# Values by seven products in sequences 2 to 7, earlier sums, gates on ScalarE's queue and look-up masks on ScalarE

## The chip, the cores and the metric

The kernel runs on one core of one Trainium2 chip. The metric is the device time of one execution in microseconds (us); several runs are given with their median, and one more execution was recorded by the hardware profiler. The engines are named as in the profile: PE (TensorE's matmuls), PEld (its weight loads), DVE (VectorE), ACT (ScalarE), POOL (GpSimd), SP (SyncE, which here only issues DMAs). Each engine works through its own instructions in the order of the program; semaphores hold it where it needs another's result. ACT also issues some DMAs, in its own order.

## The reference

Eight sequences of 1024 rows of 512 are normalized. One branch is a linear attention with three decays and a gate; the other is a feed-forward net whose weights are drawn from a table of 16 values by given indices. All is float32.

```python
xn = (x - mean) / sqrt(var + 1e-5)                 # x: (8, 1024, 512)
# attention
q = xn @ Wq                                        # 128 columns
gate = softmax(xn @ Wg)                            # 3 columns
for i in range(3):
    k = xn @ Wk[i]; v = xn @ Wv[i]                 # 128 columns each
    w = decay[i] ** max(diff - 1, 0) * (diff > 0)  # diff = column - row
    blended += gate[:, i] * (((q @ k.T) * w) @ v)
s = blended @ Wo * out_scale
# feed-forward, weights lut[idx]
h = silu(xn @ lut[gate_idx].T) * (xn @ lut[up_idx].T)   # 1376 columns
g = silu(h @ lut[down_idx].T)
out = x + s * g
```

## The kernel before

The kernel has two phases. `phase_1` makes xn transposed (stored to `xs_d`), the whole attention up to `blended` (stored to `bl_d`), and the feed-forward weights from the indices (stored to `quad_d`, `wd_d` and others). `phase_2` does the feed-forward net, the last attention matmul and the output. The change acts in phase 1; of phase 2 only one look-up (`left_weights`) uses an edited function.

**The order.** `phase_1` walks the sequences b = 0 to 8. In round b it runs side by side, as generators: `project(b)` (called `newer`), the rest of `project(b - 1)` (`ending`), `chunks(b - 1)` (`older`), the look-ups of `ffn_weights` (`build_some`), and the loads of the next sequence (`following`). A round has eight *chunk steps* k = 0 to 7, and a step has three *parts*, each beginning with `tick()`, in which issues put off by `defer(parts, ...)` come due. The order in which the generators are called is the order of every engine's instructions: `keep_order` ties it down. The order of calls in a step is: part 1: newer, older, one building step; part 2: (k < 4: ending twice), newer, one or two building steps, older, three or four building steps, (k < 4: ending); part 3: newer, older.

**project(b).** In step k it transposes one chunk of 128 rows, c = 7 - k, on PE (tile `pt`, L452) and ACT copies it to `xnT` (L453). For the coming chunks ACT normalizes (L446, L447) and gathers statistics (tile `junk`, L436, L437; for k up to 4). `values(c)` multiplies a chunk with the 387 columns of `wvg_sb` (three value matrices and the gates' three columns) in four matmuls into `pv`, which ACT copies to `v_sb` (L459, L462). The profile shows each float32 matmul as two instructions.

`features(hf)` computes q and the three k for half hf (512 rows) with seven products in place of eight, Strassen's way in Winograd's form: sums of blocks of xnT (`t1` to `t4` in `ts_`, by DVE) and of the weights (`sums_of_weights`, by GpSimd, once) are multiplied, and partial results are carried on inside PSUM: ACT copies bank pa to pb, product 6 adds onto pb, ACT copies pb to pc, products 7 and 4 add onto pc. The order is 1, 5, 6, 2, 7, 3, 4, and a product is 8 instructions of 256 columns (L520). The four banks pa, pb, pe, pc have one buffer each. Half 1 runs in steps 4 to 7 of round b (products 1 and 5 in parts 2 and 3 of step 4), half 0 in steps 0 to 3 of round b + 1 as `ending`. Three more banks (`p_c`) go round among pt, pk, psc, pv and po.

`softmax(hf)` makes the gates of a half on DVE and ACT. They must come to lie as rows repeated over all 128 partitions: they are stored to `gT_d` and read back with a broadcast into `ga` (L498). For all halves but one SP stores them two parts later, element by element (`write`, L483: 1536 words); for half 1 of sequence 0 PE transposes them, ACT copies the result to `gs` and issues the store (`turn`, L487 to L491). SP issues the read six parts after the softmax.

**chunks(b).** In step k, for chunk c = 7 - k: PE transposes k (pk, L670), ACT scales the copies (ks, L673); PE makes the scores psc (L677), DVE masks them (pr, L679) and multiplies the next chunk's gates with its q (`gated`, L652); PE adds to the state pu (L687) and makes the output po (L701: first the state's part, then pr's); ACT copies po to bl (L702), pu to R (L708) and decays pu (L715). After steps 3 and 7 ACT issues the store of bl (L704). Step 0 has no state yet, and step 7 leaves none.

**Look-ups.** `look_up` turns a tile of indices, mostly 128 x 1024, into weights. DVE makes three masks from bits 1 to 3 of the index (L220), spreads bit 0 over the word (L223, in place), makes eight leaves (L227), each a pair of table values selected by bit 0, and joins them in a tree of seven predicated copies (L244). Every instruction is one building step. The tree's other operand lies in tiles `leaf1` to `leaf3`.

Of the kernel before, what the change touches and what calls it, by code (L numbers as in the profile page):

```python
# [17 lines left out]
P = 128  # L18
# [30 lines left out]
def recurrent_block(ctx: ExitStack, tc, x, wq, wk, wv, wo, wg, decay_logits, out_scale, lut, gidx, uidx, didx, out):  # L49
# [33 lines left out]
    NQ = NO // 4  # L83
    EPS = 1e-5
# [24 lines left out]
    def more_weights(wvg_sb, wqk_sb):  # L109
        nc.scalar.dma_start(out=wvg_sb[:, :, NI * D :], in_=wg.rearrange("(c p) d -> p c d", p=P))  # L110
        for i in range(NI):
            nc.scalar.dma_start(
                out=wvg_sb[:, :, i * D : (i + 1) * D], in_=wv[i].rearrange("(c p) d -> p c d", p=P)
            )
# [36 lines left out]
    nc.gpsimd.memset(nhalf, -0.5)  # L151

# [8 lines left out]
    zero = const.tile([NI, P], F32)  # L161
# [7 lines left out]
    def tables(room):  # L169
# [8 lines left out]
        nc.gpsimd.memset(e_c, float(P))  # L178
        nc.gpsimd.memset(zero, 0.0)
# [35 lines left out]
    def look_up(build, dst, iv, rows, n):  # L215

        bits = [build.tile([P, n], U8, name=f"bit{j}", tag=f"bit{j}") for j in (1, 2, 3)]
        low = iv.bitcast(U8).rearrange("p (n four) -> p n four", four=4)[:, :, 0]
        for j in (1, 2, 3):
            nc.vector.tensor_scalar(bits[j - 1][:rows, :n], low, 1 << j, None, ALU.bitwise_and)  # L220
            yield
# [14 lines left out]
        def tree(o, level, k):  # L236
            if level == 0:
                leaf(o, k)
                yield
                return  # L240
            t = build.tile([P, n], F32, name=f"leaf{level}", tag=f"leaf{level}")
            yield from tree(o, level - 1, k)
            yield from tree(t[:rows, :n], level - 1, k + (1 << (level - 1)))
            nc.vector.copy_predicated(o, bits[level - 1][:rows, :n], t[:rows, :n])  # L244
            yield
# [3 lines left out]
    def ffn_weights(build, pool, pair_pool):  # L249
# [10 lines left out]
        def gate_up(o):  # L260
# [17 lines left out]
            yield from look_up(build, wf[:, :n], idx[:, :n], P, n)  # L278
# [40 lines left out]
        def down_tail():  # L319
# [5 lines left out]
            yield from look_up(build, wf[:m, :V], idx[:m, :V], m, V)  # L325
            defer(2, lambda: nc.sync.dma_start(out=wdt_d, in_=wf[:m, :V]))

        def down(rows, e):
# [5 lines left out]
            yield from look_up(build, t[:, : 2 * V], idx, P, 2 * V)  # L334
# [67 lines left out]
    def project(b, pools, sides, kept):  # L402
# [5 lines left out]
        xp, xnp, tp, att = pools  # L408
        wvg_sb, wqk_sb, wqs = sides
        xnT = xnp.tile([P, NV, T], F32, name=f"xnT{b}", tag="xnT")  # L410
        mean, rstd, shift = (small.tile([P, NC], F32, name=f"{k}{b}", tag=k) for k in ("mean", "rstd", "shift"))
        v_sb = att.tile([P, NC, NI * D + NI], F32, name=f"v{b}", tag="v")
        gt = v_sb[:, :, NI * D :]
# [9 lines left out]
        def statistics(c):  # L423
# [10 lines left out]
            else:  # L434
                junk = small.tile([P, V], BF16, name=f"junk{b}_{c}", tag="junk", bufs=1)
# [19 lines left out]
        def values(c):  # L455

            pv = p_c.tile([P, NI * D + NI], F32, name=f"pv{b}_{c}", tag="c")
            for v in range(NV):
                nc.tensor.matmul(  # L459
                    pv, lhsT=xnT[:, v, ts(c, P)], rhs=wvg_sb[:, v, :], start=(v == 0), stop=(v == NV - 1)  # L460
                )
            nc.scalar.copy(v_sb[:, c, :], pv)  # L462

        def softmax(hf):
# [15 lines left out]

            def write():
# [3 lines left out]
            def turn():  # L485
# [3 lines left out]
                gs = small.tile([n * NI, P], F32, name=f"gs{b}_{hf}", tag="gs", bufs=1)  # L489
# [3 lines left out]
            ga = gates[-1]  # L493
# [4 lines left out]
            defer(6, lambda: nc.sync.dma_start(out=ga, in_=there.partition_broadcast(P)))  # L498

        def features(hf):  # L500
# [14 lines left out]
            pa, pb, pe, pc = (p_a.tile([P, 2, H], F32, name=f"{r}{b}_{hf}", tag=r) for r in ("pa", "pb", "pe", "pc"))  # L515
# [12 lines left out]

            there = xs_d[b][:, :, ts(hf, H)]
            nc.vector.tensor_tensor(t1, b12, b11, ALU.subtract)  # L530
            yield
            product(pa, 1, True)
            nc.scalar.copy(pb, pa)
            nc.vector.tensor_tensor(t2, b22, t1, ALU.subtract)
            nc.sync.dma_start(out=there[:, 0:4, :], in_=xnT[:, :, ts(2 * hf, H)])
            yield
            product(pe, 5, True)
            nc.scalar.copy(c21, pe)
            nc.vector.tensor_tensor(t3, b22, b12, ALU.subtract)
            nc.sync.dma_start(out=there[:, 4:8, :], in_=xnT[:, :, ts(2 * hf + 1, H)])  # L540
            yield
            product(pb, 6)
            nc.scalar.copy(pc, pb)
            nc.scalar.copy(c12, pb)
            nc.vector.tensor_tensor(t4, b21, t2, ALU.subtract)
            defer(2, lambda: nc.sync.dma_start(out=there[:, 8:16, :], in_=ts_.rearrange("p a b u -> p (a b) u")))
            yield
            product(pa, 2)
            nc.scalar.copy(c11, pa)
            yield  # L550
            product(pc, 7)
            nc.vector.tensor_tensor(c22, pc, c21, ALU.add)
            yield
            product(pe, 3)
            nc.vector.tensor_tensor(c12, pe, c12, ALU.add)
            yield
            product(pc, 4)
            nc.scalar.copy(c21, pc)
            yield
# [25 lines left out]
        yield  # L585
        before = 2 if b == 0 else 3
        lag = 1 if b == 0 else 0
        for k in range(NC):
# [8 lines left out]
            if b == 0 and k == 0:  # L597
                warm_up(5)
            yield
            if k == NC // 2:  # L600
# [7 lines left out]
            half = softmax(1) if k == NC // 2 else iter(())  # L608
# [3 lines left out]
            if k >= lag:  # L612
# [4 lines left out]
        of_half = features(0)  # L617
        for k in range(NC // 2):
            yield
# [10 lines left out]
    def sums_of_weights(wqk_sb, wqs):  # L630

        a11, a12, a21, a22 = (wqk_sb[:, 2 * v : 2 * v + 2, ts(j, 2 * D)] for j in (0, 1) for v in (0, 1))
        s1, s2, s4 = (wqs[:, k] for k in range(3))
# [5 lines left out]
    def chunks(b, pools, kept):  # L639
# [6 lines left out]
        state = None  # L646

# [12 lines left out]
        for c in reversed(range(NC)):  # L660
# [22 lines left out]
            if not first:  # L683


                for i in range(NI):
# [3 lines left out]
                        rhs=v_sb[:, c, ts(i, D)],  # L690
# [853 lines left out]
```

## Time and profile before

| what | value |
|---|---|
| runs | 2084.59, 2086.72, 2086.76 us; median 2086.72 |
| profiled execution | 2085.11 us; span of its instructions 2083.3 us |
| granted clock of PE | 1.000 |
| PE busy, 0 to 600 us | 591.84 us |
| DVE busy, 0 to 600 us | 492.11 us |
| ACT busy, 0 to 600 us | 380.70 us |
| POOL busy, 0 to 600 us | 300.72 us |
| masks, L220 | 48 in phase 1, 0.69 us median |
| copies of pv, L462 | 64, 0.486 us each |
| store of the gates by SP, L483 | 15 |
| read of the gates, L498 | 16, 768 KB each, 7.1 us to landing (median) |

Round 2 begins at 117.68 us, round 3 at 190.87, round 8 at 550.56. A row of the timeline gives start, duration, engine, line, operation, output and inputs, shapes and count; what stands in brackets is the idle time just before, with what ended it. The ends of matmuls are modelled and overlap: what one takes from the next is read from the distance of two starts. A row of busy times gives the stretch and its length and then, for PE, PEld, DVE, ACT and POOL, the busy time and in brackets the number of instructions; at the end stand granted clock, DMA share and GB/s. A row of waits gives the engine and line that waited, what it waited for, the total, the number of times and the longest.

### The profile page before, as it was taken

What the parts mean: (1) busy time and instruction counts of PE and PEld (TensorE: products, weight loads), DVE (VectorE), ACT (ScalarE), POOL (GpSimd) and SP (SyncE); (2) the same over time, 40 slices, a digit from 0 to 9 for tenths busy, and PEclk for the clock granted to TensorE, in tenths of its full rate; (3) what the DMA queues carried; (4) which work ended last, traced back from release to release, by engine and by line L of the source; (5) the groups of instructions that cost most, each with busy time, mean ns of one, the idle gap of its engine ahead of it and who ended that gap; (6) DMA issues with size and microseconds to landing.
All of it is one profiled execution on the core that took longest, in us unless ns stands there. A gap on an engine that the chain in (4) does not pass through costs nothing.

```text
span 2083.3 us, 32914 instructions
## 1 busy us (share of the span) xinstructions
PE 2068.4 (99%) x12043; PEld 1755.3 (84%) x12043; DVE 1462.5 (70%) x2246; ACT 944.1 (45%) x2133; POOL 1043.8 (50%) x1042
## 2 busy tenths in 40 slices
PE   9999999999999999999999999999999999999999
PEld 7887888788888888897888888888978888797887
DVE  8989898788458775675577557656755765675567
ACT  4767766676444424423442442344144324423531
POOL 4554665244356446516543751755275255627442
PEclk9999999999999999999999999999999999999999
DMA  9866778756764734463464447345544734464442
GB/s 231 157 176 181 188 192 178 202 126 185 168 225 154 249 142 155 168 243 133 155 228 160 154 154 261 129 160 192 198 153 153 261 129 151 170 232 144 150 162 104
DMA packets 178494, 367.23 MB, mean 176 GB/s; under 512 B 37871, under 2 KB 113278, under 8 KB 178334
## 3 DMA queue, kind: packets, MB, share of 16 engines
q1 hardware_dynamic: 161734, 338.11, 53.0%
q10 hardware_dynamic: 12120, 12.34, 1.9%
q0 software_dynamic: 4480, 14.68, 1.7%
q8 instruction: 96, 1.57, 0.3%
q14 instruction: 64, 0.52, 0.1%
HBM read 285.36 MB, written 79.73 MB: 175 GB/s over the span
## 4 chain that ended last, share of the span: by engine, by line
PE 92%; DVE 5%; DMA 2%; issue 1%; ACT 0%; SPq 0%; POOL 0%; ACTq 0%; DVEq 0%; POOLq 0%
PE s L963 34%; PE pv L459 6%; PE sE L963 6%; PE s11d L1226 5%; PE s12d L1226 5%; PE s21d L1226 5%; PE po L701 3%; PE pd L1344 3%; PE ps L1351 3%; PE sEd L1226 2%; PE pe L520 2%; PE fs L875 2%; PE pc L520 2%; PE pa L520 2%; PE psc L677 2%; PE pu L687 1%
## 5 line engine op out<-in xcount | busy, mean ns | idle before, releaser
L963 PE MATMUL s<-xs,wq 128*128 128x256 f32 x3264 | 731.6, 379 | 0.6 <-DVE s L986 0.6
L963 PEld LDWEIGHTS s<-xs,wq 128*128 128x128 f32 x3264 | 619.3, 190 | 96.8 <-issue 7.6
L986 DVE TENSOR_TENSOR s<-s,e 128x512 f32<-128x512 f32 x136 | 95.1, 699 | 188.9 <-ACT s L985 188.9
L1315 POOL TENSOR_TENSOR cu<-cu 128x256 f32<-128x256 f32 x32 | 35.1, 1097 | 328.7 <-DVE cl L1314 328.7
L459 PE MATMUL pv<-wvg_sb,xnT 128*128 128x387 f32 x512 | 177.4, 488 | 0.0
L848 POOL TENSOR_TENSOR xs<-xs 128x256 f32<-128x256 f32 x224 | 171.1, 790 | 8.5 <-PE fr L890 4.0
L990 DVE TENSOR_TENSOR sE<-s,e 128x512 f32<-128x512 f32 x136 | 95.0, 699 | 103.2 <-PE s L963 103.1
L1058 POOL TENSOR_TENSOR u<-u,e 128x512 f32<-128x512 f32 x64 | 81.7, 1299 | 147.7 <-DVE u L1054 129.2
L981 ACT COPY e<-sE 128x512 f32<-128x512 f32 x136 | 79.6, 585 | 139.6 <-PE sE L963 137.1
L963 PE MATMUL sE<-xs,wq 128*128 128x256 f32 x544 | 139.6, 379 | 0.0
L459 PEld LDWEIGHTS pv<-wvg_sb,xnT 128*128 128x128 f32 x512 | 94.2, 190 | 53.7
L1062 POOL TENSOR_TENSOR h<-h,u 128x512 f32<-128x512 f32 x64 | 81.1, 1288 | 108.1 <-DVE u L1069 108.1
L438 POOL TENSOR_SCALAR rstd<-rstd 128x1 f32<-128x1 f32 x56 | 26.1, 467 | 209.8 <-ACT junk L437 208.8
L974 ACT COPY s<-s 128x512 f32<-128x512 f32 x136 | 77.5, 570 | 110.2 <-PE s L963 105.1
L985 ACT COPY s<-s 128x512 f32<-128x512 f32 x136 | 77.5, 570 | 97.5 <-PE s L963 97.5
L1226 PE MATMUL s12d<-wdd,z 128*128 128x128 f32 x896 | 118.4, 275 | 0.6 <-ACT s12d L1248 0.6
L963 PEld LDWEIGHTS sE<-xs,wq 128*128 128x128 f32 x544 | 103.4, 190 | 14.1
L1226 PEld LDWEIGHTS s12d<-wdd,z 128*128 128x128 f32 x896 | 109.0, 192 | 0.8 <-ACT s12d L1248 0.8
L227 DVE TENSOR_SCALAR leaf<-idx,lut_x,lut_sb 128x1024 int32<-128x1024 int32 (+2 forms) x119 | 107.7, 930 | 0.0
L656 POOL TENSOR_TENSOR qb<-ga,q_tab 128x384 f32<-128x384 f32 x56 | 75.4, 1346 | 56.1 <-DVE ga L652 26.4
L244 DVE COPY_PREDICATED leaf<-bit,leaf 128x1024 f32<-128x1024 uint8 (+2 forms) x68 | 93.5, 1375 | 1.7
L1355 POOL TENSOR_TENSOR gx<-gx,cu 128x512 f32<-128x512 f32 x32 | 40.7, 1277 | 82.0 <-DVE cu L1353 64.5
(272 smaller groups left out, 4554.4 us busy)
## 6 DMA issues: line engine op xcount, KB each, us to landing
wq<-quadd SPq DMA_DIRECT2D x112, 896.0 KB, 4.5
wdd<-wdd SPq DMA_DIRECT2D x56, 896.0 KB, 5.0
xs<-xsd SPq DMA_DIRECT2D x56, 512.0 KB, 6.4
wq<-quadd SPq DMA_DIRECT2D x48, 448.0 KB, 3.8
x<-in_x SPq DMA_DIRECT2D x64, 256.0 KB, 6.3
xsd<-xnT SPq DMA_DIRECT2D x32, 512.0 KB, 10.9
xsd<-ts SPq DMA_DIRECT2D x16, 1024.0 KB, 16.1
gx<-in_x SPq DMA_DIRECT2D x64, 256.0 KB, 6.4
```

The lines of the kernel that those rows point to most:

```text
L227: nc.vector.tensor_scalar(o.bitcast(I32), iv, lut_x[:rows, k, :], lut_i[:rows, k, 0:1], ALU.bitwise_and, ALU.bitwise_xor,)
L244: nc.vector.copy_predicated(o, bits[level - 1][:rows, :n], t[:rows, :n])
L459: nc.tensor.matmul(pv, lhsT=xnT[:, v, ts(c, P)], rhs=wvg_sb[:, v, :], start=(v == 0), stop=(v == NV - 1))
L520: nc.tensor.matmul(ps[:, j, :], lhsT=lhs[k][:, v, ts(j, D)], rhs=rhs[k][:, v, :], start=start and j == 0 and v == 0, stop=False, skip_grou ...
L848: nc.gpsimd.tensor_tensor(o, x1, x2, ALU.subtract)
L963: nc.tensor.matmul(self.t[n][:, ts(a, H)], lhsT=self.w[:, a, (0, 1, 6, 3, 4, 5, 2)[i - 1], :], rhs=self.xs[:, X_OF[self.ks[a]], D_OF[i], : ...
L981: nc.scalar.copy(self.e, self.t[3])
L986: nc.vector.tensor_tensor(self.t[1], self.t[1], self.e, ALU.add)
L990: nc.vector.tensor_tensor(self.t[3], self.t[2], self.e, ALU.add)
L1058: nc.gpsimd.tensor_tensor(o[:, n], o[:, n], other[:, n], ALU.add)
L1062: nc.gpsimd.tensor_tensor(of_h(half, n), of_h(half, n), two(other[:, n]), ALU.mult)
L1226: nc.tensor.matmul(self.t[n][:, ts(a, P)], lhsT=self.lhs[i][:, e, ts(a, P)], rhs=self.w[:, e, D_OF[i], :], start=start and a == 0 and e == ...
```

## The change

From half 1 of sequence 2 on (`by_sevens = b >= SEVENS`), the values are computed like q and k, by seven products. A half's four chunks times the padded 388 columns of `wvg_sb` are split into blocks of 256 rows, 256 of the contraction and VW = 194 columns; the sums of xnT are those of q and k, the sums of the weights are made once on GpSimd after step 0 of round 2 (with the pad column set to zero). The gates' columns now stand first, so that they are done after product 3. Products of values (v) and of q and k share the four banks, in the order v1, v5, v6, v2, v3, v7, qk1, v4, qk5, qk6, qk2, qk7, qk3, qk4. The steps are spread so: step 4 (or 0): v1 in part 1, v5 in part 2, v6 and v2 at the end of part 2 (half 0) or in part 3 (half 1); next step: v3, v7, qk1; next: v4, qk5, then qk6 and qk2; last: qk7, qk3, qk4. The main loop calls `ending` once in part 1 and twice in part 2.

The sums t1 and t2 are issued one part or more ahead of the first product, and the stores of xnT and of the sums follow v1, v5 and v6. The softmax runs after v3 and v7; after v4 the gates are turned on PE in every such half, stored by ACT, and read back by a DMA that ACT issues, one part later, in place of SP.

In every look-up (all sequences) DVE makes only the mask of bit 1. The other masks are borders: ACT computes max(index - n, 0) for n = 3, 11 and 7 into bytes, and the tree's second level takes the one of its side. The tree's level 1 writes into the unused half of the weights' tile in place of `leaf1`. Besides, `zero`, `gs` and `junk` move or shrink to make room.

```diff
-    def look_up(build, dst, iv, rows, n):
+    def look_up(build, dst, iv, rows, n, spare=None):
-        bits = [build.tile([P, n], U8, name=f"bit{j}", tag=f"bit{j}") for j in (1, 2, 3)]
+        second, *over = [build.tile([P, n], U8, name=f"bit{j}", tag=f"bit{j}") for j in range(4)]
         low = iv.bitcast(U8).rearrange("p (n four) -> p n four", four=4)[:, :, 0]
-        for j in (1, 2, 3):
-            nc.vector.tensor_scalar(bits[j - 1][:rows, :n], low, 1 << j, None, ALU.bitwise_and)
+        nc.vector.tensor_scalar(second[:rows, :n], low, 2, None, ALU.bitwise_and)
+        for j in range(3):
+            nc.scalar.activation(over[j][:rows, :n], iv, AF.Relu, bias=below[:rows, j : j + 1])
             yield
...
+            mask = second if level == 1 else over[2] if level == 3 else over[k // 4]
+            nc.vector.copy_predicated(o, mask[:rows, :n], t[:rows, :n])
...
         def softmax(hf):
+            def spread():
+                (nc.scalar if by_sevens else nc.sync).dma_start(out=ga, in_=there.partition_broadcast(P))
...
-                gs = small.tile([n * NI, P], F32, name=f"gs{b}_{hf}", tag="gs", bufs=1)
+                gs = chk.tile([n * NI, P], F32, name=f"gs{b}_{hf}", tag="ks")
                 nc.scalar.copy(gs, pg)
                 nc.scalar.dma_start(out=there, in_=gs)
...
+            if by_sevens:
+                yield
+                turn()
+                defer(1, spread)
+                yield
+                return
...
         def features(hf):
+            def product_of_v(ps, k, start=False):
+                for m in range(2):
+                    for v in range(2):
+                        nc.tensor.matmul(
+                            ps[:, m, :],
+                            lhsT=rhs[k][:, v, ts(m, P)],
+                            rhs=w_of_v[k][:, v, :],
...
+            def step(k, multiply, width, to):
+                pa, pb, pe, pc = (lambda r=r: bank(r, width) for r in ("pa", "pb", "pe", "pc"))
+                o11, o12, o21, o22 = to
+                if k == 1:
+                    multiply(pa(), 1, True)
+                    nc.scalar.copy(pb(), pa())
+                elif k == 5:
+                    multiply(pe(), 5, True)
+                    nc.scalar.copy(o21, pe())
+                elif k == 6:
+                    multiply(pb(), 6)
+                    nc.scalar.copy(pc(), pb())
+                    nc.scalar.copy(o12, pb())
+                elif k == 2:
+                    multiply(pa(), 2)
+                    nc.scalar.copy(o11, pa())
+                elif k == 7:
+                    multiply(pc(), 7)
+                    nc.vector.tensor_tensor(o22, pc(), o21, ALU.add)
+                elif k == 3:
+                    multiply(pe(), 3)
+                    nc.vector.tensor_tensor(o12, pe(), o12, ALU.add)
+                else:
+                    multiply(pc(), 4)
+                    nc.scalar.copy(o21, pc())
...
+                first = [(k, product_of_v, VW, to) for k in (1, 5, 6, 2, 3, 7, 4)]
+                steps = first[:6] + steps[:1] + first[6:] + steps[1:]
+                half = softmax(hf)
+                after = {4: half, 5: half, 7: half}
...
         for k in range(NC):
...
+            if by_sevens and k >= NC // 2:
+                next(of_half)
+            yield
+            if by_sevens:
+                if k >= NC // 2:
+                    some_of(of_half, 1)
+                yield
+                if k >= NC // 2:
+                    some_of(of_half, 2 - k % 2)
+                if k % (NC // 2) == NC // 2 - 1:
+                    of_half = features(NC // 2 // k)
+                    next(of_half)
+                yield
+                continue
...
     def phase_1():
+                    if k < NC // 2 and b > SEVENS:
+                        next(ending, None)
...
-                        for _ in range(2):
+                        for _ in range(1 if b > SEVENS else 2):
                             next(ending, None)
...
+                    if (b, k) == (SEVENS, 0):
+                        nc.gpsimd.memset(wvg_sb[:, :, NI * D + NI :], 0.0)
+                        sums_of_weights(wvg_sb, wvs, VW)
```

## The prediction

> **What bounds the kernel now.** I read the totals of the page first, then busy time by stretches, then the timeline of single chunk steps, then the waits.
>
> ```profile
> PE 2068.4 (99%) x12043; PEld 1755.3 (84%) x12043; DVE 1462.5 (70%) x2246; ACT 944.1 (45%) x2133; POOL 1043.8 (50%) x1042
> ...
> L459 PE MATMUL pv<-wvg_sb,xnT 128*128 128x387 f32 x512 | 177.4, 488 | 0.0
> ```
>
> TensorE (PE) is busy 2068.4 of 2083.3 us at full granted clock, and it never idles in front of the values (0.0). The kernel is bound by the matmuls themselves: work taken off PE shows one for one, and so does each wait put on PE. Phase 1 ends near 602 us; the edit acts there. Busy time by sequence (its round begins where its first transpose does), columns PE, PEld, DVE, ACT, POOL:
>
> ```profile
> 190.87:263.79 72.92, 71.50 (x412) 59.35 (x411) 67.38 (x83) 49.97 (x132) 38.12 (x35) 1.00 0.69 186
> ...
> 335.35:408.23 72.88, 71.42 (x412) 59.13 (x411) 54.34 (x82) 49.85 (x132) 30.90 (x34) 1.00 0.90 209
> 408.23:479.15 70.92, 70.92 (x412) 59.29 (x411) 57.48 (x78) 49.78 (x132) 34.98 (x35) 1.00 0.62 157
> ```
>
> Sequence 6 (the third row) runs without a PE gap: 70.92 us is the cost of a sequence's matmuls. The others of 2 to 7 last 73.19, 72.92, 71.56, 72.88 and 71.41: 7.4 us of waits in all. ScalarE (ACT) works 50 us of 71, VectorE (DVE) 67 in sequences 2 to 4 and 51 to 57 later. Now chunk step 4 of sequence 6, where the second half's products begin:
>
> ```profile
> 443.85 0.60 PE L452 MATMUL pt<-ident,x 128*128 128x128 f32 x4
> 444.05 0.27 ACT L702 COPY bl<-po 128x128 f32<-128x128 f32 x1 [1.38 <-PE po L701]
> ...
> 444.28 0.49 PE L670 MATMUL pk<-ident,qk 128*128 128x128 f32 x3
> ...
> 444.61 1.89 PE L520 MATMUL pa<-xnT,wqk_sb 128*128 128x256 f32 x8
> 444.71 0.48 ACT L708 COPY R<-pu 128x384 f32<-128x384 f32 x1 [0.40 <-ACT bl L702]
> 445.22 1.09 ACT L715 ACTIVATE pu<-pu,c_tab 128x128 f32<-128x128 f32 x3
> ...
> 446.23 0.59 ACT L453 COPY xnT<-pt 128x512 f32<-128x512 f32 x1
> 446.34 0.83 PE L677 MATMUL psc<-ga,qk 128*128 128x128 f32 x6
> ...
> 447.01 2.77 PE L459 MATMUL pv<-wvg_sb,xnT 128*128 128x387 f32 x8
> 447.04 0.81 ACT L447 ACTIVATE x<-x,shift,rstd 128x512 f32<-128x512 f32 x1
> ...
> 448.50 0.72 ACT L437 ACTIVATE junk<-x,mean 128x512 bf16<-128x512 f32 x1
> ...
> 449.22 0.86 ACT L673 ACTIVATE ks<-pk,k_tab 128x128 f32<-128x128 f32 x3
> ...
> 449.62 1.89 PE L520 MATMUL pe<-ts,wqs 128*128 128x256 f32 x8
> ```
>
> Two readings. PE costs are distances between starts (the ends overlap): transposes pt 0.43, pk 0.33, a q/k product 444.61 to 446.34 = 1.73, psc 0.67, values of a chunk 447.01 to 449.62 = 2.61; likewise pu 0.66, po 1.32. And ACT runs behind PE in one chain: from 0.2 us after the step's start (it waits for the last po) it works without a gap through bl, R, pu, xnT, normalization and statistics until 5.37 us into the step.
>
> **The change, part by part.**
>
> *Values by seven products, 12 halves.* A product of 194 columns is 8 instructions. One instruction of 128 columns takes 0.67/6 = 0.112, one of 256 takes 1.73/8 = 0.216; in between, 194 columns take 0.165, a product 1.32, seven 9.27. Removed: four chunks' values, 10.44. Gain 1.17 per half, 14.1 us. Each half adds one transpose of the gates, 0.43/4 = 0.11: 1.3 us. **Net -12.8 us** on PE. Bounds: at the rate per column of the 256-wide row (0.84 ns) 17.7 less 1.3; had each instruction the 256-wide row's 0.216, 12 losses of 1.66.
>
> *The wait it adds.* Product 6 accumulates on a copy (bank pb) of product 1 (bank pa). The copy is ACT's, and it is issued behind this chunk's xnT copy, normalization and statistics. Step 4 on PE: pt 0.43, product 1 1.32, pk 0.33, product 5 1.32, psc 0.67: product 6 could start at 4.07. The copy takes the place where `ks` now starts, 5.37, and lasts 0.49 (the 387-wide copy of values): 5.86. PE stands for 1.8 us, six times: 10.8. Before, product 1 stood a part later and product 6 a chunk step later, so this was hidden. At step 0 the chunk before leaves no R and no pu, `ks` starts at 3.85 and the copy ends at 4.34: 0.27, five times, 1.4. Behind the waiting product stand v2, pu and po, and for po waits bl, the next step's first ACT work, so nothing is regained. **+12.2 us**; bounds 0 (were ACT ahead) and 18 (half a microsecond more at each).
>
> *Sums sooner.* t1 and t2 move a part ahead of the products; the matmuls on them waited 0.83 us at 195.12. The xnT and ts stores follow the new steps on SP, at most a part earlier. *Gates.* Eleven stores of single words on SP vanish; SP stood 107.3 us for them (first row below), and one late gate tile cost sequence 5 its 1.96 us at 371. **-2.8 us.**
>
> ```profile
> SPq L498 <- DMA gTd<-g: 107.3, 11, 11.6
> ```
>
> (the longest wait of SP's queue between 130 and 580 us; and ACT's in the same stretch; total, times, longest)
>
> ```profile
> ACT bl L702 <- PE po L701: 82.5, 52, 5.2
> ```
>
> Now ACT's own queue must stand until the gates' store has landed, before it issues the spread. Behind it: the copies of q/k products 5, 6 and 2, and q/k product 7, early in the next step, waits for pc. Step 2 on ACT: statistics end near 5.0, copy 5.4, gs 5.6, issue 6.0. A landing takes 2.0 (shortest store of bl on that queue), 3.7 (its median) or 6.1 (the one gs before, issued 32.07, spread released 38.17). Then 1.4 of ACT until pc, against the product's start at 10.46: wait 0, 0.65 or 3.0. At step 6, without statistics, 0, 0 or 1.5. I take 0.65 six times: **+4 us**, bounds 0 and 27.
>
> The Trainium skill speaks against this part: "DMA: Bandwidth & Descriptors", section "Issuing engines are not separate DMA queues", says that another issuing engine saves only the sequencer's time. By that rule alone the move would bring 0, and ACT's wait would come on top; the row of 107.3 us says that here it is the sequencer that stood.
>
> *Masks by ScalarE.* Per look-up DVE loses two 128x1024 instructions (48 of them in phase 1, mean 1.1) and ACT gains three. No row has that Relu; Silu from SBUF takes 417 ns for 256 columns and 630 for 512, so 1024 take 1.06 as an estimate; 3.2 us a look-up, 12 look-ups in sequences 2 to 7. ACT's row above, 82.5 us of standing for po, is the cover: each half has some 10.8 us of ACT idle, of which copies (+0.8), gs and two issues take 1.7. But a group of three falls ahead of the copies of products 6 and 2, or of the next step's chain, and DVE's shift of the index must wait for the third. I price a group at 0.4 us: **+5**, bounds -4.6 (all waits that DVE still causes vanish) and +38 (nothing hidden).
>
> Against this part too there is a rule: the Trainium skill's "ScalarE: Activation LUTs", section "Rules for kernel authors", sends relu to VectorE, not to ScalarE, because VectorE is the faster. By the rows an instruction is 0.69 (median) to 1.1 (mean) there and 1.06 here, and it is DVE that works 67 of 72 us and ACT that has room. By the rule the move gives back more than it frees and the upper bound is nearer; by the rows it may win up to the 4.6.
>
> *DVE's adds.* Two adds of 388 columns per half at 0.55 (pr's 384), against 2.2 taken off each look-up: even in sum. But they crowd into steps 1 and 5. There pr may start 2.3 us after psc ends before po waits (psc ends 4.24, po's second half 7.13, pr 0.55), where it was 4.9; in the timelines of sequences 2 to 4 pr starts there 0.0 to 4.3 late. The pauses at steps 0 and 4 give DVE time back. **+2**, bounds -2 and +9. The zeroing and four sums on GpSimd (1.1 us each by its 256-wide rows, doubled at most) end over 20 us before use: 0.
>
> **Sum:** -12.8 +12.2 -2.8 +4 +5 +2 = +7.6 us on the profiled 2085.1: 2092.7. The median of the runs shown is 1.6 above that execution: **2094 us**.
>
> **Rivals.** *A, the matmuls win:* the copy of pa is ready in time, at 4.1 us into the step; then -12.8 -2.8 and little else: 2071 to 2081, say 2076. For it: PE is the only bound, the gain is sure. Against: ACT's chain to 5.37 is the same to 0.1 us in every sequence, and nothing in the diff shortens it. It decides if copy to matmul loses under 0.6 us per half. *B, even:* the wait as priced, but masks, spread and adds hidden in ACT's 82.5 us: -12.8 +12.2 -2.8 = -3.4, 2083 to 2091. *C, the spread stalls ACT:* landings of 6 us, 6 x 3.0 + 6 x 1.5 = 27 in place of 4: 2117. For it the one gs store; against it the bl stores. It decides from landings over 3.3 us at step 2. *D, the seven products don't run at 0.165 an instruction*, since the weight loads bind: against it the 128-wide rows at 0.112.
>
> **Numbers.** Forecast 0.45 (2091 to 2108), A 0.26, B 0.20, C 0.07, D 0.02. The range takes in most of A and the forecast: 2076 to 2108. What a measurement can tell from no change is about 0.2%, 4.2 us: faster 0.27, same 0.20, slower 0.53.
>
> **What would show it.** In the profile after: v rows of 194 columns 0.165 apart; PE idle or its weight load standing ahead of pb, "ACT pb", at steps 4, some 1.8 us; sequence 6 near 71 to 73 us in place of 70.92; ACT waiting on gTd<-gs; DVE's index shift (L223 now) waiting for ACT; pr (L679) late in steps 1 and 5. If the step with product 1 lasts 8.7 and not 10.5 us, the forecast is wrong and A holds.

## The result and the profile after

The changed kernel takes 2108.15 us (median of five runs, 2107.88 to 2109.87) against 2086.6 for the one before (now five runs too): a ratio of 1.0107, with an interval of 1.0096 to 1.0118. It is 21.5 us slower, where the forecast had 7.6 by its sum, and it lies just above the upper end of the range, 2108. The profiled execution has a span of 2106.4 us, 23.1 above that of before, and a mean granted clock of 0.996 in place of 1.000.

The totals of the page after (busy time, share of the span, instructions):

```profile
PE 2068.5 (98%) x12343; PEld 1801.4 (86%) x12343; DVE 1437.3 (68%) x2236; ACT 1008.1 (48%) x2220; POOL 1038.3 (49%) x1050
```

PE's busy time is the same to 0.1 us, though its work in phase 1 was cut: stretches at a lower clock filled up part of what was saved. PE's standing (span less busy time) grew from 14.9 to 37.9 us, which is the whole difference. All of it lies in phase 1: the first matmul of phase 2 starts at 609.95 us, before at 586.87. Rounds 2, 3, 5 and 6 as stretches (length, then PE, PEld, DVE, ACT, POOL; at the end clock, DMA share, GB/s):

```profile
116.79:192.92 76.13, 66.14 (x405) 60.72 (x404) 62.24 (x80) 55.20 (x137) 44.31 (x43) 0.93 0.73 201
192.92:269.58 76.66, 71.73 (x462) 67.38 (x461) 62.04 (x82) 58.22 (x144) 39.25 (x35) 0.98 0.51 166
...
344.99:416.07 71.08, 69.50 (x461) 65.69 (x460) 49.67 (x80) 59.31 (x147) 32.95 (x34) 1.00 0.58 190
416.07:491.31 75.24, 71.42 (x461) 67.38 (x460) 54.39 (x77) 58.49 (x144) 34.16 (x35) 0.98 0.47 154
```

Round 5 is the one that the forecast described: full clock and 71.08 us. The others shown are 4 to 6 us longer, with the clock below 1. Round 2 has 405 PE instructions where a full round has 461, and is still the second longest. What PE waited for between 100 and 600 us (total, times, longest):

```profile
PE po L801 <- DVE pr L779: 12.3, 8, 4.4
PE pe L557 <- DVE ts L621: 7.6, 8, 1.9
PE pc L545 <- ACT pc L577: 3.7, 4, 1.3
PE pb L557 <- ACT pb L571: 2.5, 7, 0.8
```

The kernel before, in the same stretch, has only two waits of more than a microsecond:

```profile
PE pe L520 <- DVE ts L530: 2.7, 3, 1.5
PE po L701 <- DVE pr L679: 2.4, 3, 1.5
```

So it is DVE, late with pr and with t1, that holds PE, far more than the copy the prediction had in view. Step 4 of round 5, PE and ACT alone:

```profile
379.93 0.60 PE L462 MATMUL pt<-ident,x 128*128 128x128 f32 x4
...
380.37 1.48 PE L557 MATMUL pa<-wvg_sb,xnT 128*128 128x194 f32 x8
...
381.68 0.49 PE L770 MATMUL pk<-ident,qk 128*128 128x128 f32 x3
...
382.95 1.58 PE L557 MATMUL pe<-wvs,ts 128*128 128x194 f32 x8 [0.77 <-DVE ts L621]
...
385.32 0.47 ACT L571 COPY pb<-pa 128x388 f32<-128x388 f32 x1
...
385.85 1.26 PE L557 MATMUL pb<-wvs,ts 128*128 128x194 f32 x6 [0.65 <-ACT pb L571]
```

The v products take 1.31 us from start to start (380.37 to 381.68), and the copy into pb ends 5.86 us into the step, at the predicted place. But the 1.8 us of standing is here filled in two parts, 0.77 for t1 and 0.65 for the copy: a late sum hides in front of a late copy, so the waits' list names DVE for part of what the copy would cost alone. Step 4 lasts 10.65 to 10.67 us in five of the six rounds (12.52 in round 6).

Round 2's first half, step by step (stretches):

```profile
116.79:123.68 6.89, 6.52 (x44) 5.81 (x43) 6.15 (x11) 5.16 (x14) 3.43 (x6) 1.00 1.06 364
123.68:136.45 12.77, 8.16 (x49) 7.21 (x48) 12.67 (x15) 6.88 (x18) 10.68 (x9) 0.89 0.61 122
136.45:145.38 8.93, 8.93 (x49) 8.13 (x48) 8.86 (x11) 5.39 (x15) 3.77 (x6) 0.77 1.04 139
145.38:154.41 9.03, 7.06 (x41) 6.66 (x40) 1.95 (x3) 8.67 (x19) 8.87 (x7) 0.81 0.72 220
```

Here no values are multiplied at all: those of half 1 have moved from steps 0 to 3 into steps 4 to 7, those of half 0 into the next round. Without waits the four steps hold 6.22, 6.89, 6.89 and 5.17 us of PE work, yet the main loop hands DVE the same 26 building steps as ever. In the second row DVE is busy for 12.67 of 12.77 us, and pr comes so late that PE stands 4.36 us. The four sums of weights that GpSimd makes for the values fall into this step as well, and DVE's building instructions beside them took longer than the same forms after them:

```profile
125.32 1.34 POOL L731 TENSOR_TENSOR wvs<-wvg_sb 128x388 f32<-128x388 f32 x1
125.71 1.50 DVE L233 TENSOR_SCALAR wgu<-idx,lut_x,lut_sb 128x1024 int32<-128x1024 int32 x1
...
132.96 0.80 DVE L233 TENSOR_SCALAR leaf<-idx,lut_x,lut_sb 128x1024 int32<-128x1024 int32 x1
```

Three of them took 1.50, 1.95 and 2.03 us, where the same forms took 0.80 and 1.30 us after the sums: 2.1 us more. The prediction set these sums at 0 because they end long before their use; no run moved them, so how much of the 4.36 us is theirs is not shown. In the third row PE is busy throughout, and the step is still 2 us too long: 6.89 us of work at a clock of 0.77 make 8.9. The work that left round 2 comes back behind round 7's last step: from there to phase 2 it is 53.0 us in place of 43.6.

### The profile page after: what moved, and what is told of

Its sections match the earlier page's. It is cut to its first block, busy times and chain, and to the rows that moved or that the text cites. A ratio compares the mean times of both kernels' runs of the same rounds, so it can differ in the third digit from the quotient of the medians.

```text
span 2106.4 us, 33649 instructions
## 1 busy us (share of the span) xinstructions
PE 2068.5 (98%) x12343; PEld 1801.4 (86%) x12343; DVE 1437.3 (68%) x2236; ACT 1008.1 (48%) x2220; POOL 1038.3 (49%) x1050
## 2 busy tenths in 40 slices
DMA packets 160162, 367.28 MB, mean 174 GB/s; under 512 B 19391, under 2 KB 94942, under 8 KB 159998
## 4 chain that ended last, share of the span: by engine, by line
PE 88%; ACT 5%; DVE 5%; DMA 2%; issue 1%; ACTq 0%; POOL 0%; SPq 0%; DVEq 0%; POOLq 0%
PE s L1069 33%; PE sE L1069 6%; PE s11d L1332 5%; PE s12d L1332 5%; PE s21d L1332 5%; PE po L801 3%; PE pd L1450 3%; PE ps L1457 3%; PE sEd L1332 2%; PE fs L981 2%; PE pc L545 2%; PE pe L545 2%; PE pa L545 2%; PE fr L996 1%; PE pv L469 1%; PE pu L787 1%
## 5 line engine op out<-in xcount | busy, mean ns | idle before, releaser
L1168 POOL TENSOR_TENSOR h<-h,e 128x512 f32<-128x512 f32 x64 | 81.4, 1311 | 0.0
L1164 POOL TENSOR_TENSOR e<-e,u 128x512 f32<-128x512 f32 x64 | 79.7, 1274 | 0.0
L1226 POOL TENSOR_TENSOR h<-h,u_l 128x256 f32<-128x256 f32 x64 | 67.6, 1086 | 21.8 <-DVE u_l L1121 21.8
L233 DVE TENSOR_SCALAR wgu<-idx,lut_x,lut_sb 128x1024 int32<-128x1024 int32 (+2 forms) x80 | 76.0, 957 | 0.6
```

What stands on the lines that cost most here:

```text
L233: nc.vector.tensor_scalar(o.bitcast(I32), iv, lut_x[:rows, k, :], lut_i[:rows, k, 0:1], ALU.bitwise_and, ALU.bitwise_xor,)
L1164: nc.gpsimd.tensor_tensor(o[:, n], o[:, n], other[:, n], ALU.add)
L1168: nc.gpsimd.tensor_tensor(of_h(half, n), of_h(half, n), two(other[:, n]), ALU.mult)
```

## The experiments

The theory after the traces: the loss is DVE's lateness for pr and t1, begun by round 2's light half and kept up by uneven steps, by the first bank copy's place and by masks held in ACT's queue. The rivals are single causes: the bank copy's wait alone, the masks alone, the uneven steps alone. Each expectation spells out which it tells apart; where it gives times in us, the ratio decides, since the chips differ. All kernels compute the full output. Ratios are against the kernel before on the same chip, whose medians there were 2082 to 2084 us; times of different kernels are compared through them. Building steps are instructions of the look-ups (26 to four chunk steps in both kernels). The first eight experiments are built from the changed kernel.

**Round 2's light half (e1).**

```diff
+                    elif b == SEVENS and k < NC // 2:
+                        steps = ((1, 1, 1), (1, 0, 2), (1, 1, 1), (1, 0, 1))[k]
```

> The changed kernel with fewer building steps in steps 0 to 3 of round 2 (12 in place of 26; the look-ups end later by as much). Theory 1 (thin steps): the values moved half a round later, so these four steps hold 10.4 us less PE work (some 25 us of matmuls) while DVE and ACT keep theirs; DVE bounds them (they last 37.6 us), and the PE clock drops to 0.77 to 0.89 behind the waits. Then round 2 loses 8 to 12 of its 76 us and the kernel comes to 2096 to 2101. Theory 2 (masks on ACT: DVE stands 21.9 us for the third mask, nine times, and PE for DVE): the look-ups are only put off, their waits come later; 2105 to 2110.

The four steps get 3, 3, 3 and 2 building steps, eleven in all (the expectation says 12). Measured 2102.46, ratio 1.0091 (1.0076 to 1.0106). Round 2 fell from 76.13 to 69.86 us, its first half from 37.62 to 29.00. In rounds 2 to 5 t1 now comes in time, so that there the copy's wait stands alone, 1.67 or 1.68 us each time, near the 1.8 that the forecast gave it; all six steps 4 last 10.64 or 10.65 us. For pr PE waits as long as before, in more places:

```profile
PE po L801 <- DVE pr L779: 12.5, 12, 2.0
PE pb L557 <- ACT pb L571: 7.8, 7, 1.7
```

Of the 6.3 us, 3.3 remain in the whole time by the ratio, and the two intervals overlap; round 3 grew to 78.75, why was not tried. Theory 1 had the place right and the size too large: by its ratio the run stands at 2105.6 on the chip of the first comparison, a time that theory 2 had named. Nor is DVE all that holds this half. Its steps 1 to 3 now last 7.46 or 7.47 us each, for 6.89, 6.89 and 5.17 without waits, because pu waits for ks, the end of ACT's chain of a step:

```profile
136.41 1.00 PE L787 MATMUL pu<-v,ks 128*128 128x128 f32 x6 [0.23 <-ACT ks L773]
...
143.87 1.00 PE L787 MATMUL pu<-v,ks 128*128 128x128 f32 x6 [1.96 <-ACT ks L773]
```

**The bank copy sooner (e2, e6).** In e2 all of the half's work of part 1 goes ahead of the normalization; in e6 only v1 and its copy (the hunk is e6's; e2 has `k >= NC // 2`). For half 0 the main loop calls `ending` ahead of `newer`, in e2 in all four steps, in e6 in step 0 alone.

```diff
             transpose(c)
+            if by_sevens and k == NC // 2:
+                next(of_half)
             if c > 0:
                 normalize(c - 1)
```

> The changed kernel with product v1 and its copy from bank pa to pb issued ahead of the normalization and the statistics (half 1), and ahead of the next sequence's transposes (half 0). Theory of the forecast (the copy's place in ACT's queue): the step with v1 in half 1 falls from 10.66 to 8.7 to 9.5 us, six times, step 0 by 0.3; in five of the six steps product v5 waits 0.7 to 1.9 us for DVE's sum t1 as well, under the same pause, and that part stays: 4 to 9 us less, 2099 to 2104. Theory 2 (masks): nothing, 2107 to 2109.

> The changed kernel with only product v1 and its copy to bank pb issued ahead of the normalization (half 1: step 4; half 0: step 0), the other products and the softmax where they were; the copy-first kernel before had moved those too, and ACT's exponential then stood ahead of its scaled copies ks. Ratio to the kernel before: theory of the forecast (the copy's place costs 1.7 to 1.9 us in each of six steps, in part at the same time as the late t1): step 4 between 8.7 and 10.4 us, no wait for pb left, 1.007 to 1.009. Rival (the pause only gives DVE its time, which is lost elsewhere without it): 1.010 to 1.012.

e2: 2110.9, 1.0130 (1.0115 to 1.0145). The wait for pb went, and t1 took its place (0.8 to 3.3 us in the six steps 4); besides, the softmax's work moved ahead of `ks`, and PE stood 10.8 us for ks in 11 steps: worse than both theories had it. e6: 2104.98, 1.0107 (1.0092 to 1.0123), no gain by itself, as its rival said: its PE waits are again po for pr, 12.8 us, and pe for t1, 9.8. Its steps 4 of rounds 3 to 7 are shorter by 4.0 us together, and that of round 2 is longer by 4.1.

**Masks back on VectorE (e3), and nothing but the masks (e4).**

```diff
-        nc.vector.tensor_scalar(second[:rows, :n], low, 2, None, ALU.bitwise_and)
-        for j in range(3):
-            nc.scalar.activation(over[j][:rows, :n], iv, AF.Relu, bias=below[:rows, j : j + 1])
+        for mask, bit in ((second, 2), (over[0], 4), (over[2], 8)):
+            nc.vector.tensor_scalar(mask[:rows, :n], low, bit, None, ALU.bitwise_and)
             yield
...
-    SEVENS = 2
+    SEVENS = 9
```

(the first hunk is e3, which also has the tree take these masks by level; the second is e4)

> The changed kernel with all three masks made by DVE again, the rest as it is. Theory 2 (masks on ACT cost the 22 us): 2088 to 2096. Theory 1 and the forecast's wait: DVE stands 21.9 us less for ACT but works 2 x 1.1 us more in each of 16 look-ups, and ACT's late copies (3.7 us of PE's waits for pc) go: 2103 to 2112.

> The changed kernel with no sequence by seven products: values, sums, and gates as before; what stays of the change is the masks on ACT and the moved tiles. Theory 2: most of the loss stays, 2095 to 2108. Theory 1 and the forecast: masks alone cost little where PE's steps are full, 2084 to 2091.

e3: 2106.1, 1.0108 (1.0093 to 1.0123). e4: 2085.99, 1.0010 (1.0001 to 1.0020). Both fall on the side of theory 1. Taken out of the changed kernel, the masks on ACT are worth nothing that shows; put alone into the kernel before, with the moved tiles, they cost some 0.1%: the loss is with the sevens.

**Building by step length (e5)**, since the new steps are uneven (no-wait lengths from step 4 on: 8.7, 7.8, 10.05, 7.63).

```diff
+                        if (b, k) >= (SEVENS, NC // 2):
+                            steps = ((1, 1, 4), (1, 0, 4), (2, 2, 6), (1, 1, 3))[k % 4]
```

> The changed kernel with the building steps dealt out by the new lengths of the chunk steps, from step 4 of round 2 on: 6, 5, 10, 5 per step in place of 6, 7, 7, 6, fewer of them ahead of pr (L779) in the short step and ahead of the sum t1 in the last. As a ratio to the kernel before on the same chip (the changed kernel: 1.0107). Theory U (uneven steps make DVE late for pr and t1, of which PE waits 12.3 and 7.6 us, and the clock falls behind the longer of these waits): PE's waits for pr and t1 in rounds 3 to 7 halve, 1.004 to 1.008. Rival W (DVE simply has too much work, or stands for ACT's masks): the waits move elsewhere, 1.009 to 1.012.

2107.66, 1.0119 (1.0102 to 1.0136): nothing either, as rival W said. DVE's wait for ACT's masks rose to 36.5 us.

**Three causes at once, masks on ACT (e7) and on DVE (e8).** Both have e1's, e5's and e6's edits.

> The changed kernel with the three together: fewer building steps in the thin half of round 2, the deal of building steps by length, v1 first. If the losses are these three and add up (the thin half, DVE's lateness, the copy's place), some 18 of the 22 us go: ratio 0.998 to 1.003. If DVE's or ACT's total work is the bound: 1.006 or more.

> As the one before, but all masks by DVE. If ACT's masks relieve DVE: slower than that by 0.1 to 0.4 per cent; if they make DVE stand (21.9 us in the changed kernel): as much faster.

e7: 2096.41, 1.0066 (1.0051 to 1.0081), not the sum of three causes but what its expectation named for a bound by total work. e8: 2083.92, 1.0005 (0.9995 to 1.0014), clock 1.000, phase 2 from 585.78. Now the masks are worth 0.6%, 12.5 us. Total work did not bind e7: in e8 DVE is busy longer (1485.4 us for 1446.7), and ACT was busy in e7 for only 348.30 of the 469 us from 117 to 586. Why, e7's trace shows; DVE's longest wait (first fence) and ACT's work during it (second):

```profile
160.87 0.68 DVE L224 TENSOR_SCALAR bit<-idx 128x1024 uint8<-128x1024 uint8 x1
173.59 0.69 DVE L229 TENSOR_SCALAR idx<-idx 128x1024 int32<-128x1024 int32 x1 [12.04 <-ACT bit L226]
174.20 0.55 DVE L781 TENSOR_TENSOR pr<-psc,w_tab 128x384 f32<-128x384 f32 x1
```

```profile
162.37 0.27 ACT L804 COPY bl<-po 128x128 f32<-128x128 f32 x1 [1.44 <-PE po L803]
...
169.10 0.86 ACT L775 ACTIVATE ks<-pk,k_tab 128x128 f32<-128x128 f32 x3
169.85 2.18 ACT L226 ACTIVATE bit<-idx,below 128x1024 uint8<-128x1024 int32 x2
171.93 0.58 ACT L574 COPY qk<-pe 128x512 f32<-128x512 f32 x1
172.40 1.16 ACT L226 ACTIVATE bit<-idx,below 128x1024 uint8<-128x1024 int32 x1
```

DVE has its own mask by 161.5 and its next instruction, the shift, overwrites the index that the three Relus read. They stand in ACT's queue behind a whole chunk step's copies, the first of which waits for po. DVE idles 12 us, then pr, a step's most urgent work, is late too. ACT was idle in sum, but not at that place in its order.

**How the causes add up with the masks on DVE (e9: e3 with e1; e10: e9 with e6; then e8, with e5 too).**

> The changed kernel with two things undone: look-up masks by VectorE, and 12 instead of 26 building steps in round 2's first half. Theory L (the loss is VectorE's lateness, from three causes that add up: the half round with too little matmul work, v1's place behind the transposes, masks held in ScalarE's queue): two causes gone of three, about 2095 us, round 2 near 68 us, steps 4 still near 10.65 with the wait for the first bank copy of 1.7. Theory M (once the masks are back on VectorE, the half round alone decides and the place of v1 is worth nothing): 2084 to 2088, as with all three.

> As the run before, and v1 with its bank copy moved ahead of the normalization; against the run with all parts (2083.9) it leaves out the building steps given out by step length. Theory L: the even spacing of VectorE's work over short and long steps is worth some 3 to 6 us, so 2087 to 2090, with waits for pr and t1 in steps 1 and 5. Theory M (the spacing is worth nothing, as when it was tried alone): 2082 to 2085.

| kernel | time | ratio (interval) | r2 | r3 | r4 | r5 | r6 | last step to phase 2 |
|---|---|---|---|---|---|---|---|---|
| before | 2086.6 | 1 | 73.19 | 72.92 | 71.56 | 72.88 | 70.92 | 43.6 |
| after | 2108.15 | 1.0107 (1.0096 to 1.0118) | 76.13 | 76.66 | 75.41 | 71.08 | 75.24 | 53.0 |
| e3: masks on DVE | 2106.1 | 1.0108 (1.0093 to 1.0123) | 76.34 | 75.35 | 74.22 | 71.06 | 72.68 | 53.0 |
| e9: and light half | 2095.9 | 1.0064 (1.0049 to 1.0079) | 68.44 | 75.65 | 74.25 | 72.54 | 72.94 | 53.0 |
| e10: and v1 ahead | 2090.72 | 1.0036 (1.0023 to 1.0050) | 68.51 | 75.54 | 74.27 | 70.61 | 71.49 | 53.0 |
| e8: and paced | 2083.92 | 1.0005 (0.9995 to 1.0014) | 66.64 | 73.01 | 73.42 | 69.62 | 70.18 | 53.7 |

(rounds in us of the profiled executions; in e10 and e8 product v1 of a round's step 0 stands ahead of its first transpose, so that r2 holds 1.3 us of round 3)

Each step now gives something, 0.44, 0.28 and 0.31%, though v1 ahead and pacing had given nothing alone: while one cause holds DVE or PE, removing another only moves the wait.

**The spread back on SP (e11)**, from e8, and **softer pacing (e12)**: 6, 6, 8, 6 for 6, 5, 10, 5.

```diff
-                (nc.scalar if by_sevens else nc.sync).dma_start(out=ga, in_=there.partition_broadcast(P))
+                nc.sync.dma_start(out=ga, in_=there.partition_broadcast(P))
```

> The kernel with all parts (2083.9) with the gates' spread back on SyncE's queue and nothing else changed. Theory L (the queue of the spread carries no time: the landing is 1.3 us after the issue either way): 2083 to 2085, same within 0.1%. Rival C turned round (ScalarE stands for the landing and holds copies behind it): a gain of 3 us or more, 2081 or less.

> The kernel with all parts, building steps 6, 6, 8, 6 by step in place of 6, 5, 10, 5. Theory L: the ten steps in the long step make the sum for the second-last block late in step 7 (11.66 us for 7.63 in round 3); with eight that goes and VectorE stays on time in steps 1 and 5: 2079 to 2082. Theory M (spacing is worth nothing): 2083 to 2085.

e11: 2083.42, 1.0003 (0.9993 to 1.0012), no difference; SP stood 50.0 us for the gates' landing there, and nothing was late by it. e12: 2087.64, 1.0025 (1.0015 to 1.0035): a miss for both theories, worse than e8. (The 11.66 us in its expectation hold v1 of the next round, too: without waits that step is 8.94 and not 7.63.)

**Is the saving there at all? (e13 to e16)** e8 only equals the kernel before. From it, building steps are lifted out of rounds 3 and 4 (e13); given back in round 8 (e14: two more a step); or given back in rounds 5 to 8 (e15, e16).

```diff
+                            if b in (3, 4):
+                                steps = ((1, 1, 4), (1, 0, 3), (2, 2, 5), (1, 1, 2))[k % 4]
...
-                        steps = (1, 0, 0)
+                        steps = (1, 0, 2)
```

(e13 has the first hunk, e14 both. e15 and e16 have the second, and in place of the first 23 steps to four chunk steps until round 4 and 28 from round 5, or 24 and 29.)

> The kernel with all parts (2083.9), with 23 in place of 26 building steps to four chunk steps in rounds 3 and 4. Theory L: those two rounds hold 73.0 and 73.4 us for 68.9 without waits because VectorE is full there (70.4 and 71.6 us busy of the 73); 12 steps fewer, some 10 us of VectorE, take 5 to 8 us out of them, and if the later rounds, whose VectorE is busy for 56 to 65 us of 70, take the steps up: 2076 to 2079, faster than the kernel before. Theory N (the lateness is of order, not of amount): rounds 3 and 4 keep 72 or more, 2083 to 2085. Worse if the first weights of the second phase come late: the wait at its first matmuls (0.8 us with all parts) then grows by several us.

> As the run before, with two building steps more in each chunk step of round 8, where VectorE has room. Theory L: as the run before without its wait for weights, 2075 to 2078; if nothing is late in the run before, the same as that within 1 us. Theory N: 2083 to 2085.

> The kernel with all parts, 23 building steps to four chunk steps up to round 4 and 28 from round 5, two more a step in round 8. The two runs before took 2 to 5.6 us out of the rounds up to the last chunk step (526.5 and 528.4 for 532.1) but paid 17.9 and 8.3 us at the second phase's first matmuls for weights built too late. Theory L (amount of VectorE work in rounds 3 and 4, and a date by which the weights must be built): the steps given back in rounds 5 to 7, where VectorE has some 10 us of 70 free, end the wait: 0 to 2 us of it left, 2077 to 2082. Theory N (whatever is lifted from rounds 3 and 4 comes back later in full, VectorE being the bound of the whole first phase): 2084 to 2090.

> As the run before with 24 building steps up to round 4 and 29 from round 5. Theory L: no wait for weights left, rounds 3 and 4 near 71: 2076 to 2081. Theory N: 2084 to 2090.

e13: 2102.41, 1.0096 (1.0083 to 1.0110). e14: 2094.03, 1.0053 (1.0039 to 1.0066). Chunk steps went 4 to 6 us sooner (the last began at 526.5 and 528.4, in e8 at 532.1), but phase 2 then had no weights. The waits of PE in e13 between 560 and 640 us:

```profile
PE fs L990 <- DMA wr<-wgld: 17.9, 1, 17.9
```

e15: 2086.33, 1.0016 (1.0007 to 1.0025). e16: 2087.12, 1.0023 (1.0014 to 1.0032). Rounds 3 and 5 of e15 as stretches (round 4 is like round 3, 68.80 us):

```profile
183.30:252.01 68.71, 68.71 (x461) 65.52 (x460) 63.99 (x81) 51.78 (x138) 36.37 (x35) 1.00 0.56 185
...
320.90:393.90 73.00, 69.42 (x460) 65.62 (x459) 64.55 (x86) 52.00 (x138) 37.33 (x35) 1.00 0.60 195
```

Two whole rounds run without a gap on PE, 68.71 us where the best round of before took 70.92; as soon as the building steps come back, round 5 loses 4 us (its steps 3 and 4 last 10.43 and 10.99). What PE waited for in that round (320 to 395 us):

```profile
PE pe L556 <- DVE ts L620: 2.0, 1, 2.0
PE pc L544 <- DVE qk L583: 1.5, 1, 1.5
```

DVE is late here although it is busy for only 64.55 of 73.00 us, hardly more than in round 3: here it is the order that falls short, not the time. None of the four met the 2075 to 2082 that theory L named. Rounds 3 and 4 did lose their waits as it said, but of the time theory N was right for e15 and e16: DVE's work must be done by the first matmul of phase 2, and it did not all fit beside the shorter rounds in these orders. In e8 the last chunk step begins 11.2 us sooner than before (532.09 for 543.29), and 10.1 us of that go again behind it, 9.4 of them the values that moved there. None of the orders tried beats the kernel before.

## Why the prediction was wrong, point by point

*The side was right, the size was not:* +7.6 forecast, +21.5 measured, 14 us above the named time. The side was luck as much as working: the two terms that carried the sum above zero, masks +5 and spread +4, came to nothing that shows in the changed kernel, and what made it slower stands in the term priced at +2.

*Matmuls, -12.8:* right. A gapless round costs 68.71 in e15 for 70.92, 2.2 us, some 13 for six such rounds. Rival D is out. (The bound of 17.7 does not follow from its row: 0.84 ns times 194 columns times 56 instructions is 9.13 us a half, a gain of 15.8 in all.)

*The wait for the bank copy, +12.2:* right in place and nearly in size. The copy ends at 5.86 as forecast; round 5's step 4 lasts 10.66 for 8.7 without waits (forecast: 10.5), and its step 0 8.46 for 8.04 (in e15 6.72 from the first transpose on, with v1's 1.32 ahead of it). Six times 1.96 and five times 0.42 are 13.9. So Rival A, the copy in time, did not hold; nor did Rival B, which had the same wait with everything else hidden. What the working did not see is that about half of the wait is shared with t1, and that curing the copy alone (e6) gains nothing.

*Sums sooner and gates, -2.8:* wrong in sum. The word stores went, twelve of them and not eleven (packets under 512 bytes fell from 37871 to 19391), and DVE no longer stands for late gate tiles (13.8 us in four times before, 1.2 in one after), of which one had cost round 5 its 1.96 us. But SP's standing is not by itself a cost: e11, with 50.0 us of it, is no slower than e8. The stores by words were not put back by themselves. And t1 was not sooner where it counted: PE stood 7.6 us for it in place of 2.7, as it is issued behind building steps of the step before.

*The spread on ScalarE, +4, and Rival C:* too dear. From the store's issue to the spread's it is 1.3 or 1.4 us in six of the twelve halves, where the forecast weighed landings of 2.0, 3.7 and 6.1, and 2.2 to 3.8 in the others, with ACT's other work in between. In the changed kernel's timeline (ACT's issues):

```profile
217.34 0.32 ACTq L506 DMA_DIRECT2D gTd<-gs  x1
218.69 0.33 ACTq L494 DMA_DIRECT2D ga<-gTd  x1
```

By the list of waits ACT stood 1.8 us in all for it, between 100 and 600 us. The Trainium skill's "DMA: Bandwidth & Descriptors", section "Issuing engines are not separate DMA queues", which would give the move 0, agrees with e11; the prediction had set SP's 107.3 us of standing against it.

*Masks on ScalarE, +5:* the mechanism is right and the condition was missing. In the changed kernel DVE stands for them, as said,

```profile
DVE idx L229 <- ACT bit L226: 21.9, 9, 4.3
```

but other things hold PE at the same time: e3 gives 0, and e4 0.1%. With the others cured it is 12.5 us (e7 against e8). The Trainium skill's "ScalarE: Activation LUTs", section "Rules for kernel authors", sent relu to VectorE because it is faster there (its figure is for bf16); in this case's rows the mask by Relu takes 1.15 us on ACT and the mask by a bit 0.69 (median) on DVE, but what cost was the place in ACT's queue, which neither the rule nor the sum of idle time shows.

*DVE's adds, +2, bounds -2 and +9:* this is the step that failed. It said that the change is "even in sum" for DVE and priced pr's lateness alone. By its own prices DVE gains work of 13 us and loses 26, and DVE's busy time did fall, from 1462.5 to 1437.3 us: the sum was not the trouble. It missed that the values move half a round later. Round 2's first half loses 10.44 us of PE work while DVE keeps its own, and lasts 37.62 us for 25.17 without waits; the values of the last half, now 9.4 us with the turn of the gates, return in round 8. e1 and e9 show what that half is worth: 6 to 8 us of round 2, 3 us of the whole time with the masks on ACT (within the noise), 9 with the masks on DVE (1.0108 to 1.0064). Beside that DVE stays late in the rounds behind: for pr in steps 1 and 5 of rounds 3, 4, 6 and 7, the place that the prediction named, by 6.8 us and not 2, and for t1 in all six steps 4, by 7.0 us, which it had not. In e8, with everything cured together, PE's waits for the two are 2.7 and 2.4 us.

*The clock:* the prediction took every wait at its length. Step 4 of round 6, where PE waited 1.89 us for t1 until 457.44:

```profile
455.00:457.00 2.00, 0.56 (x5) 0.29 (x3) 1.97 (x3) 1.90 (x6) 0.00 (x0) 1.00 0.68 198
457.00:459.00 2.00, 1.56 (x6) 1.56 (x7) 1.97 (x4) 1.97 (x6) 0.12 (x1) 0.75 0.00 0
459.00:461.00 2.00, 2.00 (x10) 2.00 (x10) 1.16 (x2) 1.41 (x5) 1.49 (x2) 0.50 0.00 0
461.00:463.00 2.00, 2.00 (x12) 2.00 (x12) 1.79 (x3) 0.24 (x1) 0.62 (x1) 0.90 0.00 0
```

Behind the wait the clock falls to 0.50 for a while; the three lower rows lose 0.5, 1.0 and 0.2 us, so here a wait of 1.89 cost about 3.6. Over the span 0.4% of 2106 is 8 us. That is read from the rows; no run held the waits and freed the clock. The time does not follow the clock one for one: of the five runs, that with a mean clock of 0.999 took 2107.88 us, one with 0.996 took 2108.04.

*How it adds up.* Without waits six rounds would have gained 13. Taking the rounds' lengths, the changed kernel is longer by 2.9, 3.7, 3.9, -1.8, 4.3 and 1.5 us in rounds 2 to 7 (7 to its last step) and by 9.4 behind that; it enters round 2 0.9 us sooner: 23.1.

*What stays open:* whether an order exists that keeps the 13 us. e15 shows two rounds of it, and e12 to e16 show how small shifts of DVE's steps move 2 to 18 us; neither proves that it can't be done. Open, too, is what part of the wait in round 2's step 1 belongs to the sums of weights on GpSimd.

## What to carry to other kernels

When work is moved in time, and not only made cheaper, draw up every stretch anew for every engine: a stretch that loses its matmuls but keeps its side work becomes bound by the side work (here DVE's, and below that ACT's), and the matmuls come back elsewhere. Idle time of an engine in sum is no cover for an instruction that another engine awaits; what counts is what stands ahead of it in its queue, and whether that waits too. When an experiment that cures one cause shows nothing, cure two: here v1 ahead, pacing and the masks were each worth 0 alone and 0.3 to 0.6% once the others were cured.

## What the runs showed of the hardware

A PE wait of 1.89 us was followed by some 3.4 us at half clock (0.75, 0.50 and 0.90 in stretches of 2 us), while in round 5's step 4 two gaps of 0.77 and 0.65 us left the clock at 1.00. The length of the wait alone does not decide: a wait of 2.02 us in e15 (to 360.41) and one of 3.34 us in e2 (to 157.57) left it at 1.00 in every stretch of 2 us from 357 to 365 and from 152 to 162 us. The Trainium skill's "TensorE: Matmul & The Clock Gate", Part 1, gives half clock after an idle window of some 3.4 us; in the rows above PE was still busy for 0.56 us of the 2 ahead of the drop, so here less than a full window of idleness did it. What tells these cases apart was not tried. In e13, behind the wait of 17.9 us, the stretch from 580 to 640 us has a clock of 0.83.

The Relu from 1024 words to bytes takes 1.15 us on ACT (the estimate was 1.06). The same shift of the index on DVE takes 0.69 us in most places and 2.26 at 154.76 us in the changed kernel, where a GpSimd operation of 128x896 ran from 154.38 to 156.47; other shifts beside GpSimd work took 0.69, and why was not tried.
